# The tile of 32 overflow rows in a routed feed-forward: its row load, its place among the experts, and a down product in four column tiles

## The chip, the cores and the metric

The kernel runs on one core of one Trainium2 chip. The metric is the device time in microseconds of one execution of the whole program. Before the change three runs gave a median of 414.18 us (413.87 to 414.41).

## What is computed

A decoder layer on 8 sequences of 112 tokens with 256 channels: self attention, cross attention on 375 context tokens, and a feed-forward in which each token goes to one of 8 experts beside a shared part. Layer norms follow each sum. All is float32. Cut to the part at hand:

```python
logits = x_ @ router.T
idx = jnp.argmax(logits, axis=-1)
onehot = jax.nn.one_hot(idx, 8)
u = jnp.einsum('bc,ehc->ebh', x_, up)
g = jnp.einsum('bc,ehc->ebh', x_, gate)
ye = jnp.einsum('ebh,ech->ebc', jax.nn.silu(g) * u, down)
y = jnp.einsum('ebc,be->bc', ye, onehot)
ys = jax.nn.silu(x_ @ w_gate_s.T) * (x_ @ w_up_s.T) @ w_down_s.T
x = layernorm(x + y + ys)
```

Here x_ has 896 rows of 256, and the hidden size is 512.

## The kernel before

The two attentions take the first 318 us or so of the profiled execution and are not touched. Then comes the feed-forward, whose order is written out by hand in the table LAST: a string of short words, each of which is a function that issues a few instructions. Every engine runs its own instructions in that order, so the table is the order of each queue. The pool of each tile name has a fixed number of buffers, and a new tile waits until the oldest of its name is free.

**The experts.** The rows of x are scattered to a DRAM array xs_d in which each expert owns a stretch of 896 rows; xs_d is filled by indirect DMAs. Each expert's first 128 rows make a tile (tiles 0 to 7). Rows beyond 128 of one expert are few: with at most 32 of them, of one expert, they make tile 8, a `SmallTile` of 32 rows, whose expert (`whose_i`) and first row (`row_i`) VectorE works out (`beyond`, the word x). With more rows the program goes into a tail under a condition, which this input does not take.

Each tile has three pieces:

- `turn` (words A0 to A8, line 820): two PE transposes of its rows, and a copy by ScalarE.
- `gate_up` (B0 to B8): 16 matmuls for gate and up, then silu on ScalarE and a product on VectorE, which gives hT. For tile 8 (line 862) the rows are the stationary side, and the four quarters of the hidden size go to four column tiles of PE, at output partitions 0, 32, 64 and 96.
- `down` (C0 to C8): four matmuls that add up in PSUM, then VectorE adds x (line 850), and SP writes the rows to a DRAM array y_d (line 851). For tile 8 the hidden part is first turned by one transpose (line 876) and a ScalarE copy (hTs, line 878).

`down(t)` also calls `load_expert(t + 4)`: SP issues the three weight loads of the tile four places on (wg, wu, wd, lines 600 to 602, 512 KB each, four buffers each). For tile 8 SP first loads `whose_i` and `row_i` into registers (line 805), then issues the load of the 32 rows (line 894), then the weights of that expert. All these DMAs stand on SP's one queue, in order.

**After the experts.** i0 writes the place of every token to DRAM, and i1 reads it back in another layout (line 694). Y0 to Y6 gather y_d by these places with indirect DMAs on GpSimd (line 697); Y0 waits for all writes to y_d. g0 and g1 are silu and product of the shared part's two halves (lines 639 and 640), h3 is a last piece of it. D0 to D6 are the down products of the shared part, of 128 tokens each: four matmuls, the gathered rows added by VectorE (line 648), and the statistics of the norm. They take turns with two PSUM buffers. Z0 to Z6 apply the norm on ScalarE and write the result.

`ident` is a 128x128 unit matrix, made by GpSimd at the start.

Of the kernel before, what the change touches and what calls it, by code (L numbers as in the profile page):

```python
# [8 lines left out]
F32 = mybir.dt.float32  # L9
I32 = mybir.dt.int32  # L10
AF = mybir.ActivationFunctionType
ALU = mybir.AluOpType
AX = mybir.AxisListType

P = 128
# [29 lines left out]
LAST = """  # L45
S0 a2- E0 a1+ S1 T00+ T01- E1 b0- T02+ S2 F1 T10- W0 T12- E2 b1- U0+ T11+ S3 T20+ T21- a0- F2 E3
T22+ W1 V0 F3 T30- T32- F4 T31- U1- r V1 f1 R a3- f2 b2+ f3 f4 p h2 P b3- h1 L0 L1 g0 h0 A0 x A1 L2
B0 i0 B1 C0 A2 C1 A3 B2 A4 B3 C2 A5 B4 C3 C4 A6 B5 A7 B6 A8 C5 B7 C6 B8 C7 g1 i1 C8 Y0 h3 Y1 Y2 Y3
D0 Y4 Y5 D1 Y6 D2 Z0 D3 D4 Z1 D5 Z2 Z3 Z4 D6 Z5 Z6
"""  # L50


# [1 line left out]
def decoder_layer(  # L54
# [8 lines left out]
    nc = tc.nc  # L63
    B, S, D = x.shape
    NT = B * S
# [8 lines left out]
    E, _, H = upT.shape  # L74
    KH = H // P
# [6 lines left out]
    SMALL = 32  # L82

    const = ctx.enter_context(tc.tile_pool(name="const", bufs=1))
# [4 lines left out]
    V, A, G = nc.vector, nc.scalar, nc.gpsimd  # L89
# [4 lines left out]
    def t_tile():  # L94
        return ps_t.tile([P, 512], F32, tag="pt", name="pt")

    def m_tile():
        return ps_m.tile([P, 512], F32, tag="mm", name="mm")
# [25 lines left out]
    load = nc.sync.dma_start  # L124
# [53 lines left out]

    ident = const.tile([P, P], F32, name="ident")
    make_identity(nc, ident)  # L180
    mhalf = const.tile([P, 1], F32, name="mhalf")
    G.memset(mhalf, -0.5)

# [28 lines left out]
    xs_d = tc.dram_tile([E * NT, D], F32, name="xs_d")  # L212
    y_d = tc.dram_tile([E * NT, D], F32, name="y_d")
# [42 lines left out]
    def product(out_, pairs):  # L256
        for i, (lhsT, rhs) in enumerate(pairs):
            nc.tensor.matmul(out_, lhsT, rhs, start=(i == 0), stop=(i == len(pairs) - 1))  # L258
# [313 lines left out]
    for s in range(B):  # L572
        if s + 1 < B:
            load_context(s + 1)
        if s in (1, 2):
            load(
                out=(xs_d if s == 1 else y_d)[:, :].rearrange("(t p) d -> p t d", p=P),
                in_=fill_sb.unsqueeze(1).to_broadcast([P, E * NT // P, D]),
# [14 lines left out]
    fp = ctx.enter_context(tc.tile_pool(name="fp", bufs=2))  # L593
    wp = ctx.enter_context(tc.tile_pool(name="wp", bufs=4))

    def load_weights(u, g, d):
        wg = wp.tile([P, KD, H], F32, tag="wg", name="wg")
        wu = wp.tile([P, KD, H], F32, tag="wu", name="wu")
        wd = wp.tile([P, KH, D], F32, tag="wd", name="wd")
        load(out=wg, in_=g.rearrange("(k p) h -> p k h", p=P))  # L600
        load(out=wu, in_=u.rearrange("(k p) h -> p k h", p=P))
        load(out=wd, in_=d.rearrange("(k p) c -> p k c", p=P))
        return wu, wg, wd
# [38 lines left out]
    def last_sum(i):  # L642


        h, n = (raw["u"], i) if i < FT else (hS1, i - FT)
        ps = m_tile()
        product(ps[:, :D], [(h[:, hc, bass.ts(n, P)], swd[:, hc, :]) for hc in range(KH)])
        V.tensor_tensor(r[:, i, :], ps[:, :D], r[:, i, :], ALU.add)
        stats(mv[:, i, :], r[:, i, :])
        rstds[i] = rstd_of(mv[:, i, 1:2])  # L650

    def last_norm(i):
        shift = mv[:, i, 0:1]
        V.tensor_scalar(shift, shift, rstds[i], -1.0, ALU.mult, ALU.mult)
        A.activation(r[:, i, :], r[:, i, :], AF.Identity, bias=shift, scale=rstds[i])
        load(out=out[bass.ts(i, P), :], in_=r[:, i, :])

    raw_pieces = {}
# [3 lines left out]
    def small_tile(name, shape=None, dt=F32):  # L662
        return fc.tile(shape or [S, B], dt, name=name)
# [26 lines left out]
    def places_out():  # L690
        load(out=place_d[:, :].rearrange("(b s) o -> s (b o)", s=S), in_=place_i)

    def places_in():
        load(out=place_2, in_=place_d[:, :].rearrange("(i p) o -> p (i o)", p=P))

    def from_places(i):
        G.indirect_dma_start(
            out=r[:, i, :],
            out_offset=None,
            in_=y_d[:, :],  # L700
            in_offset=bass.IndirectOffsetOnAxis(ap=place_2[:, i : i + 1], axis=0),
            bounds_check=E * NT - 1,
            oob_is_err=False,
        )
# [50 lines left out]
    row_i = small_tile("row_i", [1, NOV], I32)  # L755
# [48 lines left out]
    def value(at, most):  # L804
        return nc.sync.value_load(at, min_val=0, max_val=most)
# [4 lines left out]
    class ExpertTile:  # L810
# [32 lines left out]
        def down(self):  # L843
            ps = m_tile()
            n = self.x.shape[0]
            product(
                ps[:n, :D], [(self.hT[:, hc, 0:n], self.w[2][:, hc, :]) for hc in range(KH)]
            )
            y = fp.tile([P, D], F32, tag="y", name="y", bufs=3)
            V.tensor_tensor(y[:n], ps[:n, :D], self.x, ALU.add)  # L850
            load(out=y_d[bass.ds(self.rows, n), :], in_=y[:n])

    class SmallTile(ExpertTile):
# [17 lines left out]
            V.tensor_tensor(h, ug[:, 0, 0:P], h, ALU.mult)  # L871
            self.h = h

        def down(self):
            pt = t_tile()
            nc.tensor.transpose(pt[:, 0:P], self.h, ident)
            self.hT = fp.tile([P, KH, SMALL], F32, tag="hTs", name="hTs", bufs=1)
            A.copy(self.hT.rearrange("p k n -> p (k n)"), pt[:, 0:P])
            super().down()

    tiles = [ExpertTile(t * NT, xs[:, t, :]) for t in range(E)]
    tiles.append(SmallTile(None, xs[0:SMALL, E, :]))
# [5 lines left out]
    def load_expert(t):  # L888
        if t < E:
            tiles[t].w = load_weights(upT[t], gateT[t], downT[t])  # L890
        else:
            e = value(whose_i[0:1, 0:1], E - 1)
            tiles[t].rows = value(row_i[0:1, 0:1], E * NT - P)
            load(out=tiles[t].x, in_=xs_d[bass.ds(tiles[t].rows, SMALL), :])
            tiles[t].w = load_weights(upT[e], gateT[e], downT[e])

    for t in range(4):
        tiles[t].w = weights.pop(t)

    def down(t):  # L900
        tiles[t].down()
        if t + 4 <= E:
            load_expert(t + 4)
# [7 lines left out]
    for t in range(E + 1):  # L911
        raw_pieces[f"A{t}"] = lambda on, t=t: tiles[t].turn()
        raw_pieces[f"B{t}"] = lambda on, t=t: tiles[t].gate_up()
        raw_pieces[f"C{t}"] = lambda on, t=t: down(t)
    raw_pieces["i0"] = lambda on: places_out()
    raw_pieces["i1"] = lambda on: places_in()
    for i in range(NTT):
        raw_pieces[f"Y{i}"] = lambda on, i=i: from_places(i)
        raw_pieces[f"D{i}"] = lambda on, i=i: last_sum(i)
        raw_pieces[f"Z{i}"] = lambda on, i=i: last_norm(i)  # L920
# [79 lines left out]
```

## Time and profile before

| what | value |
|---|---|
| median of three runs | 414.18 us (413.87 to 414.41) |
| the profiled execution | 414.01 us |
| its span in the trace | 412.2 us |
| granted TensorE clock, mean | 0.995 |
| busy: PE, VectorE, ScalarE, GpSimd | 398.8, 235.9, 194.0, 73.4 us |
| share of PE in the chain that ended last | 84% |
| tile 5's gate product starts / ends | 367.34 / about 369.13 us |
| last down product of the experts ends | 388.5 us |
| last instruction that is counted as busy starts | 406.18 us |

The times in the last three rows are from the start of the span. In the timeline a line gives the start in us, the length in us, the engine, the line of the code, the instruction, the tile that it writes and those it reads, shapes and the number of records; in brackets stands the time for which the engine was idle just before, and what released it. A float32 matmul leaves two records. PE is the matmuls and PEld the weight loads. An engine with a q behind its name is that engine's queue of DMA issues; the length is that of the issue, not of the transfer. The end of a transfer is given apart, as the time from issue to landing. The chain that ended last is followed back from the last instruction, at each step to what released it.

### The profile page before, as it was taken

What the parts mean: (1) busy time and instruction counts of PE and PEld (TensorE: products, weight loads), DVE (VectorE), ACT (ScalarE), POOL (GpSimd) and SP (SyncE); (2) the same over time, 40 slices, a digit from 0 to 9 for tenths busy, and PEclk for the clock granted to TensorE, in tenths of its full rate; (3) what the DMA queues carried; (4) which work ended last, traced back from release to release, by engine and by line L of the source; (5) the groups of instructions that cost most, each with busy time, mean ns of one, the idle gap of its engine ahead of it and who ended that gap; (6) DMA issues with size and microseconds to landing.
All of it is one profiled execution on the core that took longest, in us unless ns stands there. A gap on an engine that the chain in (4) does not pass through costs nothing.

```text
span 412.2 us, 8511 instructions
## 1 busy us (share of the span) xinstructions
PE 398.8 (97%) x3353; PEld 312.1 (76%) x3353; DVE 235.9 (57%) x665; ACT 194.0 (47%) x486; POOL 73.4 (18%) x109
## 2 busy tenths in 40 slices
PE   8999999999999999999999999999999999999991
PEld 8877768867886887688678867867857559998681
DVE  1164685588458666855784586489567533211362
ACT  1242475356636554654557286677468331201203
POOL 3030012113012200221030113104101440000082
PEclk9999999999999999999999999999999999999998
DMA  7990497199010001000000100000596132977133
GB/s 249 311 254 2 150 369 237 42 378 330 4 40 0 2 2 39 0 2 13 27 2 2 39 0 3 1 2 2 179 376 213 32 114 57 322 258 255 31 89 96
DMA packets 40382, 46.61 MB, mean 113 GB/s; under 512 B 4005, under 2 KB 33458, under 8 KB 40338
## 3 DMA queue, kind: packets, MB, share of 16 engines
q1 hardware_dynamic: 39074, 43.93, 33.2%
q0 software_dynamic: 720, 1.84, 1.5%
q8 instruction: 28, 0.46, 0.4%
q10 hardware_dynamic: 544, 0.26, 0.2%
q14 instruction: 16, 0.13, 0.1%
HBM read 28.42 MB, written 17.60 MB: 112 GB/s over the span
## 4 chain that ended last, share of the span: by engine, by line
PE 84%; DMA 6%; issue 3%; POOL 2%; SPq 1%; DVE 1%; ACT 1%; POOLq 0%; DVEq 0%
PE mm L258 47%; PE pt L495 10%; PE sc L447 7%; PE mm L506 4%; PE sc L258 4%; PE sc L346 4%; PE mm L382 3%; PE pt L375 3%; DMA xs<-xs_d 2%; POOL xs_d L675 1%; DMA wk<-in_w_qkv 1%; DMA wu<-in_upT 1%; PE pt L249 1%; DMA r<-y_d,place 1%; DMA xs_d<-xres,place_i 1%
## 5 line engine op out<-in xcount | busy, mean ns | idle before, releaser
L465 ACT ACTIVATE ex<-ex,nm 112x375 f32<-112x375 f32 x128 | 76.5, 599 | 48.8 <-DVE nm L461 48.0
L461 DVE CUSTOM_DVE_ANT_0 ex<-sc,cap 112x375 f32<-112x375 f32 x128 | 63.7, 543 | 10.1 <-PE sc L447 9.3
L495 PEld LDWEIGHTS pt<-ident,ex 112*125 112x125 f32 x384 | 50.8, 188 | 17.1 <-issue 9.2
L495 PE MATMUL pt<-ident,ex 112*125 112x112 f32 x384 | 55.4, 276 | 0.1
L254 ACT COPY exT<-pt 125x448 f32<-125x448 f32 x58 | 29.4, 526 | 26.1 <-PE pt L495 25.9
L368 POOL TENSOR_TENSOR pr<-pr,den 112x896 f32<-112x896 f32 x16 | 26.9, 1683 | 78.5 <-DVE den L367 41.8
L239 POOL TENSOR_TENSOR rs<-rs,mhalf 112x1 f32<-112x1 f32 (+1 forms) x23 | 12.7, 552 | 151.9 <-DVE rs L238 151.4
L258 PE MATMUL mm<-wv,xT_sb 128*112 128x512 f32 x64 | 31.1, 608 | 0.0
L447 PE MATMUL sc<-kc,qz 32*112 32x375 f32 x256 | 29.8, 519 | 0.1
L258 PE MATMUL mm<-wo,aoT 128*112 128x256 f32 x128 | 29.0, 380 | 0.0
L258 PE MATMUL mm<-xT_sb,wq 128*128 128x224 f32 x128 | 27.9, 363 | 0.0
L254 DVE COPY exT<-pt 125x448 f32<-125x448 f32 x38 | 23.6, 622 | 6.3 <-PE pt L495 5.8
L258 PE MATMUL mm<-xT_sb,wk 128*128 128x224 f32 x128 | 26.9, 354 | 0.3 <-DMA wk<-in_w_qkv 0.3
L258 PEld LDWEIGHTS mm<-xT_sb,wq 128*128 128x128 f32 x128 | 24.0, 195 | 3.3 <-issue 3.2
L258 PE MATMUL mm<-wxv,cT 128*125 128x256 f32 x96 | 25.6, 389 | 0.0
L258 PEld LDWEIGHTS mm<-wo,aoT 128*112 128x112 f32 x128 | 22.0, 177 | 4.5 <-DVE aoT L254 0.2
L258 PEld LDWEIGHTS mm<-xT_sb,wk 128*128 128x128 f32 x128 | 23.7, 190 | 2.0 <-PE mm L258 0.6
L465 ACT ACTIVATION_READ_ACCUMULATOR ex<-ex,nm 112x1 f32 x128 | 23.9, 187 | 0.0
L258 PE MATMUL mm<-cT,wxk 128*128 128x375 f32 x64 | 23.2, 486 | 0.0
L506 PE MATMUL mm<-exT,vc 125*32 125x112 f32 x768 | 21.7, 261 | 0.0
L254 DVE COPY prT<-pt 112x448 f32<-112x448 f32 x16 | 9.8, 620 | 20.7 <-PE pt L375 20.7
L355 DVE TENSOR_REDUCE mx<-sc 112x8 f32<-112x896 f32 x16 | 17.4, 1088 | 5.9 <-PE sc L346 5.4
(160 smaller groups left out, 645.0 us busy)
## 6 DMA issues: line engine op xcount, KB each, us to landing
xs_d<-fill_sb SPq DMA_DIRECT2D x1, 7168.0 KB, 24.0
y_d<-fill_sb SPq DMA_DIRECT2D x1, 7168.0 KB, 24.7
wg<-in_gateT SPq DMA_DIRECT2D x9, 512.0 KB, 6.4
wu<-in_upT SPq DMA_DIRECT2D x9, 512.0 KB, 7.3
wd<-in_downT SPq DMA_DIRECT2D x9, 512.0 KB, 8.8
cT<-in_ctxT SPq DMA_DIRECT2D x8, 375.0 KB, 3.3
wv<-in_w_qkv SPq DMA_DIRECT2D x2, 512.0 KB, 8.2
wo<-in_w_out SPq DMA_DIRECT2D x1, 1024.0 KB, 13.6
```

Source lines behind the costliest of these rows:

```text
L239: G.tensor_tensor(rs[:n], rs[:n], mhalf[:n], ALU.pow)
L254: (V.tensor_copy if on == "+" else A.copy)(dst, src)
L258: nc.tensor.matmul(out_, lhsT, rhs, start=(i == 0), stop=(i == len(pairs) - 1))
L346: nc.tensor.matmul(sc[:S, j, bass.ts(c, S)], qT[rows, 4 * g + c, self.tok], kT[rows, 4 * g + c, self.tok], start=True, stop=True,)
L355: V.tensor_reduce(self.mx, scv, AX.X, ALU.max)
L368: G.tensor_tensor(pr, pr, den.unsqueeze(3).to_broadcast([S, 2, 4, S]), ALU.mult)
L375: nc.tensor.transpose(pt[:S, bass.ts(c, S)], self.pr[g][:, j, c, :], ident[:S, :S])
L447: nc.tensor.matmul(sc[i // 2][:S, i % 2, :S2], self.qz[rows, par, c, :], kc[rows, c, :], start=True, stop=True,)
L461: V.tensor_tensor_reduce(ex[:, i, :], self.sc[g][i // 2][:S, i % 2, :S2], cap, -1.0, BIG, ALU.add, ALU.min, nm[:, i : i + 1],)
L465: A.activation(ex[:, i, :], ex[:, i, :], AF.Exp, bias=nm[:, i : i + 1], scale=-1.0, accum_out=den[:, i, g % 2 : g % 2 + 1],)
L495: nc.tensor.transpose(pt[:JT, bass.ts(i, S)], self.ex[g][:, i, bass.ts(t, JT)], ident[:S, :S])
L506: nc.tensor.matmul(av[32 * i : 32 * i + 32, 0:S], vcs[self.b % 2][:, t, 4 * c + i, bass.ds(32 * par, 32)], self.exT[2 * c + par][:, t, bas ...
```

## The change

Four things are changed, all of them on tile 8, and one word of the shared part moves with them.

1. The load of the 32 rows, with the register load of `row_i`, is a word of its own, L3, behind C0.
2. In the table, A8 goes ahead of B6 and B8 ahead of C6; the turn of the hidden part is a word of its own, y0, behind C6; g1 goes behind A8, and i1 ahead of C7.
3. The down product of tile 8 is the word y1, between B7 and C7. Its four matmuls no longer add up in one PSUM area of 32 rows: each goes to its own 32 output partitions. ScalarE copies the four parts to a tile of the name y.
4. C8 is one matmul that adds up the four parts, with a 0/1 matrix of 128x32 (`fourth`) which VectorE makes at the start by adding up four column blocks of `ident`. Its sum has x added and is written as before.

```diff
-B0 i0 B1 C0 A2 C1 A3 B2 A4 B3 C2 A5 B4 C3 C4 A6 B5 A7 B6 A8 C5 B7 C6 B8 C7 g1 i1 C8 Y0 h3 Y1 Y2 Y3
-D0 Y4 Y5 D1 Y6 D2 Z0 D3 D4 Z1 D5 Z2 Z3 Z4 D6 Z5 Z6
+B0 i0 B1 C0 L3 A2 C1 A3 B2 A4 B3 C2 A5 B4 C3 C4 A6 B5 A8 g1 B6 C5 A7 B8 C6 y0 B7 y1 i1 C7 C8 Y0 h3
+Y1 Y2 Y3 D0 Y4 Y5 D1 Y6 D2 Z0 D3 D4 Z1 D5 Z2 Z3 Z4 D6 Z5 Z6
...
+    fourth = const.tile([P, 32], F32, name="fourth")
+    V.tensor_reduce(fourth, ident.rearrange("p (c m) -> p m c", m=32), AX.X, ALU.add)
...
-        def down(self):
+        def turn_hidden(self):
             pt = t_tile()
             nc.tensor.transpose(pt[:, 0:P], self.h, ident)
             self.hT = fp.tile([P, KH, SMALL], F32, tag="hTs", name="hTs", bufs=1)
             A.copy(self.hT.rearrange("p k n -> p (k n)"), pt[:, 0:P])
-            super().down()
+
+        def down_parts(self):
+
+            ps = m_tile()
+            for hc in range(KH):
+                nc.tensor.matmul(
+                    ps[32 * hc : 32 * hc + 32, :D], self.hT[:, hc, :], self.w[2][:, hc, :],
+                    start=True, stop=True,
+                )
+            self.parts = fp.tile([P, D], F32, tag="y", name="yp", bufs=3)
+            A.copy(self.parts, ps[:, :D])
+
+        def down(self):
+            ps = m_tile()
+            nc.tensor.matmul(ps[:SMALL, :D], fourth, self.parts, start=True, stop=True)
+            y = fp.tile([P, D], F32, tag="y", name="y", bufs=3)
+            V.tensor_tensor(y[:SMALL], ps[:SMALL, :D], self.x, ALU.add)
+            load(out=y_d[bass.ds(self.rows, SMALL), :], in_=y[:SMALL])
...
             e = value(whose_i[0:1, 0:1], E - 1)
-            tiles[t].rows = value(row_i[0:1, 0:1], E * NT - P)
-            load(out=tiles[t].x, in_=xs_d[bass.ds(tiles[t].rows, SMALL), :])
             tiles[t].w = load_weights(upT[e], gateT[e], downT[e])
...
+    def load_beyond():
+        tiles[E].rows = value(row_i[0:1, 0:1], E * NT - P)
+        load(out=tiles[E].x, in_=xs_d[bass.ds(tiles[E].rows, SMALL), :])
+
+    raw_pieces["L3"] = lambda on: load_beyond()
...
+    raw_pieces["y0"] = lambda on: tiles[E].turn_hidden()
+    raw_pieces["y1"] = lambda on: tiles[E].down_parts()
```

## The prediction

> **What bounds the kernel now.** I read the page's busy shares first: PE is busy for 398.8 of 412.2 us. A busy share is a mean over stages, so I then read the chain that ended last, cut to the stage that the change touches (from 360 us), and last the timeline of that stage, first PE alone, then all engines.
>
> PE's timeline, whose columns are start, length, engine and line, instruction, and the idle time before it. "x16" counts records, two for each fp32 matmul:
>
> ```profile
> 375.82 0.28 PE L820 MATMUL pt<-ident,xs 32*128 32x32 f32 x2 [0.95 <-DMA xs<-xs_d]
> 376.03 1.99 PE L258 MATMUL mm<-wd,hT 128*128 128x256 f32 x8
> 377.86 1.95 PE L258 MATMUL sc<-xsT,wg 128*128 128x128 f32 x16
> ...
> 381.43 1.89 PE L258 MATMUL mm<-wd,hT 128*128 128x256 f32 x8
> 383.25 0.65 PE L862 MATMUL sc<-wg,xsT 128*32 128x128 f32 x16
> 383.71 0.62 PE L862 MATMUL sc<-wu,xsT 128*32 128x128 f32 x16
> 384.26 1.99 PE L258 MATMUL mm<-wd,hT 128*128 128x256 f32 x8
> 386.09 0.27 PE L876 MATMUL pt<-ident,h 128*128 128x128 f32 x1
> 386.72 1.91 PE L258 MATMUL mm<-wd,hTs 128*32 128x256 f32 x8 [0.35 <-ACT hTs L878]
> 388.56 1.56 PE L258 MATMUL sc<-x2T,swu 128*128 128x384 f32 x4
> ```
>
> The differences of the starts are what each piece costs PE: an expert's gate and up 3.57, its down product 1.73 to 1.83, a turn 0.21, the small tile's gate 0.46 and up 0.55, its down product 1.84. PE stands still for 0.95 (the 32 rows) and 0.35 us (the turned hidden rows). Both are taken away by the change.
>
> But PE is not what ends this stage. The chain, whose columns are start, length and what:
>
> ```profile
> 389.11 1.49 DMA y_d<-y
> ...
> 391.56 2.82 DMA r<-y_d,place
> ...
> 394.96 7.19 PE mm L258 x32
> ```
>
> After the last down product the chain leaves PE: VectorE adds x, the 32 rows are written (landed 390.60), GpSimd gathers, VectorE adds (to 394.92), and only then does PE get a PSUM buffer for the third sum (D2) (394.96). PE fills that time with h3, D0 and D1 and idles just 0.15 us. So an earlier PE is worth nothing unless the write of the small tile's rows **lands** earlier; I work out that landing.
>
> The links on both sides of it, from the timeline of all engines:
>
> ```profile
> 381.63 0.60 ACT L839 ACTIVATE sg<-sc 128x512 f32<-128x512 f32 x1 [5.23 <-PE sc L258]
> 382.26 0.69 DVE L841 TENSOR_TENSOR hT<-sc,sg 128x512 f32<-128x512 f32 x1 [3.77 <-ACT sg L839]
> ...
> 386.75 0.33 SPq L851 DMA_DIRECT2D y_d<-y  x1
> ...
> 388.67 0.41 DVE L850 TENSOR_TENSOR y<-mm,xs 32x256 f32<-32x256 f32 x1 [0.82 <-PE mm L258]
> ```
>
> An expert's hidden rows are ready 1.57 us after PE ends its up product (381.43 to 382.95, and 0.05 to start); before, C6 (1.82) covered this for B7.
>
> **The change, part by part.** PE's order after B5, which ends at 370.92, becomes A8, B6, C5, A7, B8, C6, y0, B7, y1, C7, C8.
>
> Removed: the 0.95 and the 0.35 us. The rows' load, with its register load, moves from SP's queue ahead of tile 8's weights to behind C0's. There SP is idle until C2's write at 360.53 apart from C1's write and tile 5's weights; these go 1.4 us later (the same items took SP from 369.86 to 371.28). Tile 5's last landings are 359.5 (up) and 360.9 (down); PE wants them from 367.34. Cost nothing; without that cover, 1.4. g1 moves ahead of B6: ScalarE 1.05 and VectorE 1.22 us between 371.9 and 374.2, where before both idle from 372.4 to 374.9; nothing, or up to 1 us on hT6, which C6 wants only after 377. The 0/1 matrix is one VectorE instruction near 1.5 us, of some 0.3 by the nearest small rows (h, 128x128: 0.29); VectorE then idles 6.57 us until 8.63: nothing. The place load goes ahead of C7's write; it took 2.4 us and has more time than before.
>
> The down product in four column tiles: 8 records of 256 columns. The nearest row is L862, where 16 records of 128 columns in four column tiles took 0.46 to 0.55: so about 0.5, and 1.84 if the tiles ran one after another. With the sum (one matmul, two records at 0.216: 0.43) 0.93 in place of 1.84. The Trainium skill (TensorEngine Tiling (Array Packing), Key Properties) speaks against it: a change of tiling mode drains the array. The row: around L862 weight loads idle 0.33 and 0.20. By the row and the rule alike y1 may be 0.5 longer, 1.0 in all, and it still ends inside the wait that follows, so the sum does not move.
>
> **New wait 1: tile 8's up weights.** B8 comes 6.6 us earlier (376.65 for 383.25), its weights hardly do:
>
> ```profile
> L601 SPq DMA_DIRECT2D wu<-in_upT x1: 378/378/378, 372.2 to 372.2; - x1
> ...
> DMA to landing us min/median/max: 6.8/6.8/6.8
> ```
>
> 372.17 + 6.8 = 378.97, and B8's up half wants them at 377.11. SP issues them 1.4 us sooner (the second register load and the rows' DMA are gone). If landing followed issue: 377.55. If it follows the backlog of the queue: 378.97 less 0.08 for the 32 KB: 378.9. The small transfers say backlog: the 128 KB y at 368.82 landed after 6.7 us and the 32 KB rows, at 370.73, after 4.95, against 1.5 to 1.8 elsewhere. In half-microsecond windows the DMA share was 0.54 to 0.62 from 369.5 to 371 and 0.53 at 373, so an earlier issue can fill a little. I take 378.5, near the backlog's end; PE starts 0.14 after a landing (375.68 to 375.82): a wait of 378.64 - 377.11 = 1.53, bounds 0 (the transfers run at the full rate seen later, 390 GB/s) and 1.93. Behind it on PE stand C6, y0, B7 and all the rest.
>
> **New wait 2: hT7.** Between B7 and C7 only y1 (0.5) is left to cover 1.57: 1.07 us idle.
>
> **New wait 3: the small tile's write behind C7's.** The rows' place is a register, so the write can overlap any other; the changed program makes SP wait for the landing of C7's write (its semaphore stands in the write's list of waits). It did so before too, but then C7's write at 386.75 had landed after 1.8, at 388.55, 0.5 us before the small y was ready at 389.08. Now C7 ends only 0.43 before the small product: the two landings follow one another. The skill (DMA: Bandwidth & Descriptors, Two DMAs through the same engine are not ordered) says that this wait cannot be dropped, and (Anatomy of one DMA, fitted on GpSimd's path) that each transfer has about 2.0 us fixed: by the rule the second landing costs 2.08, by the row 1.49. I use the row; the rule would add 0.6.
>
> **Sum.** A8 371.13, B6 374.71, C5 376.44, A7 376.65, B8's gate 377.11, wait to 378.64, up 379.19, C6 381.02, y0 381.23, B7 384.80, hT7 at 386.37, C7 388.17, small sum 388.60 (before: 388.56). The 2.2 us taken off PE are given back as waits. Then y7: 388.17 + 0.2 + 0.42 + 0.04 = 388.83 issued, + 1.8 = 390.63 landed; small write + 0.2 (SP's moves) = 390.83, + 1.49 = 392.32 landed, against 390.60. **+1.7 us.** The gather and all after it follow unchanged: third sum (D2) at 396.7. The profiled execution took 414.01 us (span 412.2 and 1.8 around it): 415.7. The median of the runs, 414.18, becomes 415.9.
>
> **The rivals.** (a) The weights come in time (full DMA rate). Then C7 ends at 386.64, the small write lands at 390.8: +0.2, 414.4. For it: 390 GB/s at 376 to 378. Against it: 133 to 250 GB/s at 370.5 to 373.5.
> (b) Faster: the small write is not held back by C7's (it lands before, or the wait is not on it) and weights come in time. Then 387.07 + 0.18 + 0.42 + 0.04 + 1.49 = 389.2: -1.4, 412.8. It decides once the two writes overlap in full and the wait for weights is under 0.6. Against it: the semaphore in the list.
> (c) Slower still: full backlog (+0.4), and the second write takes 1.8 like its neighbours (+0.3): 416.6.
> (d) The column tiles do not run side by side: y1 1.84 ends 0.3 after hT7: 416.2, inside the forecast.
>
> **Chances.** Measurement tells about 0.2% (0.83 us) from no change. Forecast with (d) 0.58, of which nearly all is slower; (a) 0.25, same; (b) 0.05, faster; (c) 0.12, slower. So slower 0.68, same 0.28, faster 0.04. The range runs from (a) less 0.3 of scatter (runs before span 0.54 us) to just above (c).
>
> **What would show it.** The 0.95 and 0.35 idle times gone; PE idle ahead of L865's second half, put to DMA wu; about 1.1 us ahead of C7 on hT; the small y_d write starting some 2 us after C7's, not after its own y; about 1.8 us of PE idle ahead of the third sum (D2). Wrong would be: no wait for wu8 (then 414.4), or a small write issued beside C7's.

## The result, and the profile after

The change makes the kernel slower, by about a quarter of a per cent. Nine runs of the changed kernel gave a median of 415.31 us (414.89 to 415.94), and nine of the kernel before, on the same chip, 414.18 us: a ratio of 1.0027 with a 95% interval of 1.0015 to 1.0038, so +1.1 us (0.6 to 1.6). The profiled execution took 415.78 us with a span of 414.0, which is +1.77 on the profiled execution of before. The forecast was +1.7, inside the range; why the profiled pair shows nearly all of it and the medians only two thirds is the main thing that the experiments had to settle.

PE's timeline of the changed kernel, in the stage that the change touches (columns as before; L865 is tile 8's gate and up, L879 the turn of its hidden rows, L887 the down product in four column tiles, L896 the sum of the parts):

```profile
371.08 0.31 PE L823 MATMUL pt<-ident,xs 32*128 32x32 f32 x2
...
376.72 0.38 PE L823 MATMUL pt<-ident,xs 128*128 128x128 f32 x2
377.57 0.64 PE L865 MATMUL sc<-wg,xsT 128*32 128x128 f32 x16 [0.47 <-ACT xsT L827]
378.85 0.64 PE L865 MATMUL sc<-wu,xsT 128*32 128x128 f32 x16 [0.63 <-DMA wu<-in_upT]
379.43 1.99 PE L261 MATMUL mm<-wd,hT 128*128 128x256 f32 x8
...
385.03 0.64 PE L887 MATMUL mm<-wd,hTs 128*32 128x256 f32 x8
386.51 1.99 PE L261 MATMUL mm<-wd,hT 128*128 128x256 f32 x8 [0.84 <-DVE hT L844]
388.44 0.62 PE L896 MATMUL mm<-yp,fourth 128*32 128x256 f32 x2
388.99 1.56 PE L261 MATMUL sc<-x2T,swu 128*128 128x384 f32 x4
...
396.68 3.50 PE L261 MATMUL mm<-swd,raw_u 128*128 128x256 f32 x15 [1.39 <-DVE r L651]
```

The waits for the rows (0.95) and for the turned hidden rows (0.35) are gone, and three others are there: at B8 for weights, 0.84 ahead of C7, and 1.39 ahead of the third sum (D2), where PE stood still for 0.09 before (from 394.87 to 394.96; the prediction's 0.15 is a little large). h3 starts at 388.99; it started at 388.56 before. So what PE was relieved of has been given back by the time it reaches h3. How long the wait at B8 is can't be read from its brackets alone. From the turn at 376.72 to C6 at 379.43 it is 2.71 us, and 1.32 in executions without any wait there (shown below): 1.39 us.

The chain that ended last, of the same execution:

```profile
370.54 8.27 DMA wu<-in_upT
...
386.51 2.01 PE mm L261 x8
388.52 0.02 issue
388.55 0.43 DVE y L853
388.98 0.02 issue
389.00 1.70 DMA y_d<-y
...
390.91 1.50 DMA y_d<-y
...
393.28 2.82 DMA r<-y_d,place
...
396.68 7.19 PE mm L261 x32
```

Here is the loss. Two landings stand one behind the other: C7's 128 rows (389.00 to 390.70), then the 32 rows, issued only at 390.91, although VectorE had them ready (the add of line 898 started at 389.10 and took 0.41). They land at 392.41; before they landed at 390.60. Gather, add and D2 follow.

### The profile page after: what moved, and what is told of

Read it like the earlier page. It is cut to its first block, busy times and chain, and to the rows that moved or that the text cites. A ratio compares the mean times of both kernels' runs of the same rounds, so it can differ in the third digit from the quotient of the medians.

```text
span 414.0 us, 8520 instructions
## 1 busy us (share of the span) xinstructions
PE 398.9 (96%) x3355; PEld 312.2 (75%) x3355; DVE 236.3 (57%) x666; ACT 194.5 (47%) x487; POOL 73.4 (18%) x109
## 3 DMA queue, kind: packets, MB, share of 16 engines
q0 software_dynamic: 720, 1.84, 1.5%
## 4 chain that ended last, share of the span: by engine, by line
PE 85%; DMA 5%; issue 3%; POOL 2%; DVE 1%; SPq 1%; ACT 1%; POOLq 0%; DVEq 0%
PE mm L261 47%; PE pt L498 10%; PE sc L450 7%; PE sc L261 5%; PE mm L509 4%; PE sc L349 4%; PE mm L385 3%; PE pt L378 3%; DMA wu<-in_upT 2%; POOL xs_d L678 1%; PE mm L136 1%; DMA y_d<-y 1%; PE pt L252 1%; DMA r<-y_d,place 1%; DMA xs_d<-xres,place_i 1%
```

## The experiments

The theory: the loss is made by the wait for hT7 and the two landings in sequence, and what PE saves lies behind the gather and is worth nothing. The first rival: the late weights of tile 8 make it. The second: the down product in parts and its sum make it.

For each trace I use one length, **the stage**: from the start of tile 5's gate product to the start of D2. It is 396.68 - 367.41 = 29.27 us in the changed kernel and 394.96 - 367.34 = 27.62 before. What follows it, from D2 to the start of the last counted instruction, takes 11.21 or 11.22 us in every trace of this document, so nothing of the change is lost or won there.

**Tile 8's weights ahead of tile 7's.** SP issues the two sets of weight loads in the other order, so that tile 8's come sooner and tile 7's later:

```diff
-            load_expert(t + 4)
+            load_expert({3: 8, 4: 7}.get(t, t + 4))
```

> The changed kernel, but tile 8's weights are asked for after C3 and tile 7's after C4, the other way round. Theory of three waits: the 0.47 and 0.63 us for which PE idles ahead of the two halves of B8 are waits for tile 8's weights; they go, the small write lands 1.1 us earlier (about 391.3 in place of 392.4), time 415.3 - 1.1 = 414.2. Tile 7's up weights then land at about 378.8, ahead of B7 at 380.2. Rival (the weights cost nothing that ends later; the time is lost in the early load or in the column tiles): 415.3. Rival (the 0.47 ahead of the gate half is for the copy of A7, not for weights): only 0.6 comes back, 414.7.

Measured: 415.01 us, 1.0023 (1.0013 to 1.0033) against before. From PE's timeline of this kernel:

```profile
376.74 0.38 PE L823 MATMUL pt<-ident,xs 128*128 128x128 f32 x2
377.05 0.64 PE L865 MATMUL sc<-wg,xsT 128*32 128x128 f32 x16
377.51 0.62 PE L865 MATMUL sc<-wu,xsT 128*32 128x128 f32 x16
378.06 1.99 PE L261 MATMUL mm<-wd,hT 128*128 128x256 f32 x8
...
385.15 1.99 PE L261 MATMUL mm<-wd,hT 128*128 128x256 f32 x8 [0.84 <-DVE hT L844]
```

B8 does not wait (378.06 - 376.74 = 1.32), nor does B7 for tile 7's weights, yet the time stayed about where it was: 0.2 us less than the changed kernel by the two ratios, with some 0.6 either way. The expectation missed. The first rival can't be the main cause: with no wait for weights at all the kernel is still 0.95 us slower than before.

**The small rows written to a fixed place.** The address is then no register, and SP does not have to wait for C7's write. The last 32 rows of y_d, which C7's write does not touch, take the rows, so this kernel leaves tile 8 out of the result.

```diff
-            load(out=y_d[bass.ds(self.rows, SMALL), :], in_=y[:SMALL])
+            load(out=y_d[E * NT - SMALL : E * NT, :], in_=y[:SMALL])
```

> The changed kernel, but the small tile's 32 rows go to a fixed place, the last 32 rows of y_d, so that its write need not wait for C7's; the rows of tile 8 are left out of the result. Theory of three waits: the small write is issued at about 389.55 in place of 390.91 and lands by 391.1 to 391.3 in place of 392.4; time 415.3 - 1.2 = 414.1. Rival (the two writes lie beside each other anyway, or the gather waits for something else): 415.3.

Measured: 414.21 us, 1.0008 (1.0000 to 1.0016), some 0.8 us less than the changed kernel. The chain of this kernel:

```profile
388.33 0.56 PE mm L896 x2
388.89 0.02 issue
388.91 0.42 DVE y L898
389.33 0.02 issue
389.35 1.48 DMA y_d<-y
```

The write goes out as soon as its own add is done, 0.53 us behind C7's (388.82), and one landing of 1.48 is left in the chain. PE does not idle ahead of D2. The wait that the prediction named is real: the edit takes it away, with SP's register moves for the address (0.2 us), and touches nothing else. The wait of 0.84 for hT7 is still there. The run also refutes the prediction's rival (b): that the write isn't held back.

**The sum and its write ahead of C7.** The same remedy with the whole result kept; one word moves in the table:

```diff
-... C6 y0 B7 y1 i1 C7 C8 Y0 h3
+... C6 y0 B7 y1 i1 C8 C7 Y0 h3
```

> The changed kernel, but the small sum and its write (C8) stand ahead of C7 in the table; the column tiles stay. Theory of three waits: the sum lies in the 0.84 us for which PE waits for hT7, the small write lands at about 388.8, and C7's, which now comes last, at about 390.9 in place of 392.4: 1.5 us less than the changed kernel of the same call. Rival (the order of the two writes does not matter, only how much stands behind C7): about the same as the changed kernel, or 0.4 less for the sum that is hidden.

Measured: 413.88 us, 0.9994 (0.9983 to 1.0005), beside 1.0028 for the changed kernel, run again (below): -1.4 us, close to the 1.5 expected. PE's timeline:

```profile
383.49 0.64 PE L887 MATMUL mm<-wd,hTs 128*32 128x256 f32 x8
384.62 0.62 PE L896 MATMUL mm<-yp,fourth 128*32 128x256 f32 x2 [0.49 <-ACT yp L892]
385.17 1.99 PE L261 MATMUL mm<-wd,hT 128*128 128x256 f32 x8
```

SP's two writes, from the timeline of all engines (L899 the 32 rows, L854 C7's):

```profile
385.71 0.34 SPq L899 DMA_DIRECT2D y_d<-y  x1
...
387.65 0.34 SPq L854 DMA_DIRECT2D y_d<-y  x1
```

The sum (0.55) stands where PE waited for hT7, so that wait is gone, and the small write has landed long before C7's is issued. One landing is left, C7's. The edit undoes waits 2 and 3 together.

**Only the early rows.** The kernel before, with the rows' load as a word behind C0 and nothing else:

```diff
-B0 i0 B1 C0 A2 C1 ...
+B0 i0 B1 C0 L3 A2 C1 ...
```

> The kernel before, with one part of the change alone: the 32 rows and their register load behind C0. Theory of three waits: the 0.95 us of PE idle at A8 goes and nothing new comes, since B8 stays late (about 382.3, its weights there by 379), C8 keeps its place, and C7's write has landed before the small y is ready: 414.2 - 0.95 = 413.2. Rival (the early load costs SP's queue or the transfers what it brings): 414.2.

Measured: 413.27 us, 0.9990 (0.9982 to 0.9998): -0.41 us, less than half of the 0.95 of the profiled execution. In the trace the rows are waited for no more and nothing else is late. So the 0.95 is not what an execution pays on average.

**Both kernels again.** 

> The changed kernel once more, as the measure for the others of this call. Expected 1.0027 of before as in its first runs. If it comes out nearer 1.0038, the upper end of that interval, the swap of the weights and the other single edits had gained more than their medians seemed to say.

> The kernel before once more, for a trace of the same call. The time from the last counted instruction to the end of the span was 6.0 us in its first trace and 6.3 to 6.8 in those of the single edits. If it is 6.3 to 6.8 here, that is a difference of chips or of executions, not of the edits; if it is 6.0 again, an earlier end is partly given back by the last stores.

Measured: 415.24 us (1.0028, 1.0018 to 1.0037) and 413.84 us (0.9994, 0.9980 to 1.0008). A second trace of the same programs answers what the early rows left open. From PE's timeline, first the kernel before:

```profile
373.39 1.95 PE L258 MATMUL sc<-xsT,wu 128*128 128x128 f32 x16
375.34 0.28 PE L820 MATMUL pt<-ident,xs 32*128 32x32 f32 x2
```

and the changed one:

```profile
377.06 0.38 PE L823 MATMUL pt<-ident,xs 128*128 128x128 f32 x2
377.37 0.64 PE L865 MATMUL sc<-wg,xsT 128*32 128x128 f32 x16
378.01 0.64 PE L865 MATMUL sc<-wu,xsT 128*32 128x128 f32 x16
378.59 1.99 PE L261 MATMUL mm<-wd,hT 128*128 128x256 f32 x8
...
385.68 1.99 PE L261 MATMUL mm<-wd,hT 128*128 128x256 f32 x8 [0.84 <-DVE hT L844]
...
395.85 1.35 PE L261 MATMUL mm<-swd,raw_u 128*128 128x256 f32 x5 [1.39 <-DVE r L651]
```

The 0.95 is gone: the rows landed 3.8 us after their issue, not 5.0. The wait at B8 has shrunk from 1.39 to 1.53 - 1.32 = 0.21: the up weights landed after 7.2 us, not 8.3. The 0.84 and the 1.39, on the other hand, are the same to 0.01 us. **Two kinds of wait have been mixed**: those for transfers at 370 to 379 us, which come and go from execution to execution, and those that the order makes, which stand in each. What the second trace of before was meant to tell came out too: from the start of the last counted instruction to the end of the span it was 6.0 us in the first trace and is 6.6 here, in the range of the single edits (6.3 to 6.8), so it differs between two executions of one program as much as between edits.

**Only the order.** The changed kernel's order up to B7, without parts: tile 8's down product adds up in PSUM as before, and C8 is ahead of C7.

```diff
-... C6 y0 B7 y1 i1 C7 C8 Y0 h3
+... C6 y0 B7 i1 C8 C7 Y0 h3
...
-            nc.tensor.matmul(ps[:SMALL, :D], fourth, self.parts, start=True, stop=True)
+            product(
+                ps[:SMALL, :D], [(self.hT[:, hc, :], self.w[2][:, hc, :]) for hc in range(KH)]
+            )
```

> The changed kernel's order with the down product of before: in place of y1 stands the small tile's whole down product (four matmuls that add up, no parts, no 0/1 sum), so its write goes ahead of C7's. Theory of three waits: 1.84 us of PE work covers the wait for hT7 in full, C7 ends at about 388.6 as now, but the small write lands at about 389 and C7's, behind it, at 390.95 in place of 392.4: 415.3 - 1.45 = 413.9, so the column tiles and their sum at the end are a loss. Rival (the column tiles save PE time that counts): more PE work, 415.3 + 0.9 = 416.2.

Measured: 413.96 us, 1.0007 (0.9998 to 1.0015). It is 0.9 us faster than the changed kernel, less than the 1.45 expected. PE's timeline:

```profile
383.95 1.91 PE L261 MATMUL mm<-wd,hTs 128*32 128x256 f32 x8
385.80 1.99 PE L261 MATMUL mm<-wd,hT 128*128 128x256 f32 x8
```

C7 does not wait; tile 8's product of 1.85 us covers hT7 by itself. B8 waited 0.77 us for weights in this trace.

**Only the parts.** The order before, with y0, y1 and the sum one behind the other after C7:

```diff
-... C0 L3 A2 ... A6 B5 A8 g1 B6 C5 A7 B8 C6 y0 B7 y1 i1 C7 C8 Y0 h3
+... C0 A2 ... A6 B5 A7 B6 A8 C5 B7 C6 B8 C7 g1 i1 y0 y1 C8 Y0 h3
...
             e = value(whose_i[0:1, 0:1], E - 1)
+            load_beyond()
```

> The kernel before in its own order, with one part of the change alone: the small tile's down product on four column tiles, the parts copied by ScalarE and added up by the 0/1 matrix, all behind C7. Theory: 0.64 for the parts, 0.49 of PE idle for the copy (as in front of the sum in the kernel with the sum first) and 0.55 for the sum stand in place of 1.84, so the small write lands 0.1 to 0.2 us earlier: the same as before within 0.2. Rival (the column tiles give their full saving, 1.84 - 0.93): 0.9 less than before. Rival (the copy on the path costs more than is saved): 0.4 more.

Measured: 414.07 us, 1.0002 (0.9989 to 1.0014), no difference. PE's timeline:

```profile
387.17 0.64 PE L887 MATMUL mm<-wd,hTs 128*32 128x256 f32 x8 [0.35 <-ACT hTs L881]
388.30 0.62 PE L896 MATMUL mm<-yp,fourth 128*32 128x256 f32 x2 [0.49 <-ACT yp L892]
388.85 1.56 PE L261 MATMUL sc<-x2T,swu 128*128 128x384 f32 x4
```

From 387.17 to 388.85 it is 1.68 us, beside 1.84 for the product that adds up. The four column tiles run side by side (0.64 in all), but the copy of the parts (0.49) and the sum (0.55) eat nearly all of it. The prediction's rival (d) falls. So does the second rival, in the changed order too: sum first (parts) and order only (no parts) both have the write of the 32 rows ahead of C7's, and the stage, without the wait at B8, is 26.42 us with parts and 26.59 without.

**Swap and sum first together.** The two edits of the first and third experiment in one kernel, run twice:

> As the kernel with the sum first, and tile 8's weights asked for ahead of tile 7's. If the waits for weights count in full, 1.1 to 1.4 us less than the kernel with the sum first. If, as the swap alone suggested by its median, they do not, the same as that one within 0.3.

> The kernel with the swap of weights and the sum first once more, beside the last one on the same chip. Its first ratio was 0.9975 [0.9963, 0.9988], that of the covered kernel 0.9985 [0.9976, 0.9994]; their traces put the third sum of the shared part within 0.15 us of each other. Expected between the two, 0.998.

Measured: 413.30 us, 0.9975 (0.9963 to 0.9988), and 413.18 us, 0.9978 (0.9969 to 0.9987). This is the version that beats both: about 1.0 us less than before, about 2 less than the changed kernel. On the kernel with the sum first it gains 0.7 to 0.8, between the two forecasts (1.1 to 1.4, or nothing beyond 0.3). Of PE's waits only the one ahead of D2 (0.48) and that for the parts (0.49) are left.

**hT7 covered by work.** The swap, tile 8's product without parts, and B7 ahead of C6, so that two down products stand between B7 and C7:

```diff
-... A8 g1 B6 C5 A7 B8 C6 y0 B7 y1 i1 C7 C8 Y0 h3
+... A8 g1 B6 C5 A7 B8 B7 y0 C6 i1 C8 C7 Y0 h3
```

> All three waits taken away: rows early, tile 8's weights ahead of tile 7's, B7 right behind B8, then C6 (it covers hT7), the small tile's down product in one piece (no column tiles), and C7 and its write last. Theory of three waits: no idle on PE to the end of C7 at about 386.9, its write lands at 389.2 against 390.6 before, third sum of the shared part 1.4 earlier against a before with the 0.95 wait for the rows, 0.5 to 1.0 earlier against one without: 1.0 to 1.4 less than before, and less than the kernel with the swap and the sum first by 0.2 or so. Rival (the end is set by the transfers of the last stores, which grow as the rest ends earlier): no more than 0.5 less than before.

Measured: 413.34 us, 0.9985 (0.9976 to 0.9994). PE does not idle until D2. Faster than before by 0.6, which is less than expected and near the rival's 0.5, and not to be told from the kernel above by its interval.

**The same with the weights in their usual order,** and B8 late enough for them; hT has three buffers for it, and sg gives one up (two), since with three of each the pool `wp` would want 48 KB per partition where 46.03 are left:

```diff
-... A8 g1 B6 C5 A7 B8 C6 y0 B7 y1 i1 C7 C8 Y0 h3
+... A8 g1 B6 A7 B7 B8 C5 y0 C6 i1 C8 C7 Y0 h3
```

> As the covered kernel, but with the weights asked for in their usual order and B8 put behind B7 (C5 and C6 behind both), so that tile 8's weights have until about 378.5 to land; hT has three buffers and sg two. Theory of three waits: PE has the same work as the covered kernel and idles 0.3 us at most ahead of B8: within 0.3 of 0.9985 of before. If B8 waits there, up to 0.5 more.

Measured: 414.20 us, 1.0007 (0.9997 to 1.0017), a miss. PE's timeline:

```profile
374.76 0.38 PE L823 MATMUL pt<-ident,xs 128*128 128x128 f32 x2
375.88 2.05 PE L261 MATMUL sc<-xsT,wg 128*128 128x128 f32 x16 [0.73 <-ACT xsT L827]
```

B8 waits for no weights, but tile 7's turn now stands right ahead of its own gate product: ScalarE's copy of the turned rows, which other pieces used to cover, is exposed, and it starts only at 375.46, since ScalarE takes tile 6's silu first (from 374.96). From turn to gate it is 1.12 us instead of the 0.31 of a turn.

## Why the prediction came out as it did

All traces in one table. "Transfer wait" is the time at A8 for the rows, or at B8 for the weights (A7's start to C6's start, less 1.32); the fourth column is the stage without it. The time against before is worked out from the ratio. Where D2's first record follows D1's without a gap, its start is taken from the chain.

| kernel | stage, us | transfer wait | stage less wait | time against before, us |
|---|---|---|---|---|
| before, two traces | 27.62, 26.67 | 0.95, 0 | 26.67, 26.67 | |
| changed, two traces | 29.27, 28.10 | 1.39, 0.21 | 27.88, 27.89 | +1.1, +1.2 |
| weights swapped | 27.87 | 0 | 27.87 | +0.95 |
| fixed place | 27.84 | 1.29 | 26.55 | +0.3 |
| sum first | 26.61 | 0.19 | 26.42 | -0.25 |
| rows early | 26.55 | 0 | 26.55 | -0.4 |
| order only | 27.36 | 0.77 | 26.59 | +0.3 |
| parts only | 27.81 | 1.23 | 26.58 | +0.1 |
| swap and sum first, two traces | 26.44, 26.42 | 0, 0 | 26.44, 26.42 | -1.0, -0.9 |
| hT7 covered | 26.63 | 0 | 26.63 | -0.6 |
| hT7 covered, weights in order | 27.53 | 0 | 27.53 | +0.3 |

The fourth column repeats to 0.02 us in the three programs that were traced twice: what the order makes is the same in both. By it the change costs 27.88 - 26.67 = 1.21 us. To that comes the mean of one transfer wait less that of the other.

Point by point:

- **Direction and mechanism: right.** The prediction said that PE's saving is given back as waits, and that the small write lands later because the two landings follow one another. Two edits that undo this, each in its own way, shorten the stage less wait by 1.33 (fixed place) and 1.46 us (sum first). The first leaves the wait for hT7 in and still comes below before (26.55 and 26.67), so the loss goes with the second landing alone. What the wait for hT7 costs while two landings follow is not shown: no run takes it away alone.
- **New wait 3: right in size.** The first landing took 1.70 (taken: 1.8), the second 1.50 (1.49). The Trainium skill's fixed cost of about 2.0 us for each transfer (DMA: Bandwidth & Descriptors, Anatomy of one DMA) would, as an estimate, have made the second 2.08; the row was the better guide.
- **New wait 2: right, a little large.** 0.84 in place of 1.07, in all four traces with this order. hT7 came when the sum had it, 5.14 us after B7's start, but y1 began 0.09 later behind B7 (3.66 us for 3.57) and took 0.64 and not 0.5. For the drain at a change of tiling mode, which the skill names without a price (TensorEngine Tiling (Array Packing), Key Properties), the prediction allowed y1 up to 1.0; nothing of that size is seen, the 0.09 and the 0.14 together being 0.23.
- **New wait 1 and the 0.95 removed: the step that failed.** In the execution that was profiled the working holds: 1.39 us at B8 (predicted 1.53, all of it ahead of the up half; 0.54 of it stood ahead of the gate half), the small rows landed at 392.41 (392.32), D2 at 396.68 (396.7), the execution at 415.78 (415.7). But the sum then added the +1.7 of one execution to the median of all. It took the rows' 0.95 out of before and put 1.53 for the weights in, a net of +0.58, as if both were constants. Second traces show 0 and 0.21, and that the first pair of executions came within 0.1 us of the forecast is in part luck: the second pair ran 414.07 and 415.25, which is +1.18.

  All traces together give a fairer mean. Five have the changed order and the usual order of loads as far as B8 (both of the changed kernel, fixed place, sum first, order only): their wait for the weights is 0.77 in the mean. Three have the rows' load in its old place (both of before, parts only): 0.73. As an estimate from these eight, the two waits nearly cancel, and the change comes to 1.21 + 0.04 = 1.25 us; measured are +1.1 (0.6 to 1.6). The run times are less sharp. By them the rows are worth some 0.3 us (rows early: -0.41, of which 0.12 is in the stage less wait), and the weights 0.2 (swap against the changed kernel) to 0.8 (swap and sum first against sum first), each with 0.3 to 0.7 either way.
- **Rival (a), weights in time, +0.2:** wrong in its number for the same reason. From the start of the stage, the small rows land after 23.61 us with swapped weights. Against the first trace of before, with its 0.95, that is 0.35 later (23.26), near what (a) gave; against the second, without it, 1.30 later (22.31). The kernel with weights in time measured +0.95.
- **Early load and g1: right.** SP's queue has tile 5's weights later and PE does not wait for them, and neither hT6 nor the rows are waited for.

What stays open: ahead of the stage and behind the last counted instruction executions differ as well. The stage starts between 366.95 and 367.81, and from the start of that instruction to the end of the run it is 7.83 to 8.54 us. In the two traces of before this hides the 0.95: the second began the stage 0.47 later and took 0.55 more at the end (8.38 for 7.83), and the two ran 414.01 and 414.07. No run here takes either apart. Whether the end grows when the rest is done sooner is not shown: the two traces of swap and sum first, with stages alike to 0.02, have 8.40 and 8.04.

Some edits also gained less than the stage says. With the mean waits above, weights swapped, fixed place, rows early and order only fall 0.3 to 0.5 us short, all others 0.2 or less. These four were timed beside one set of runs of before, with a median of 413.74 where the other sets have 413.96 to 414.25. That before waited less for its rows in that set would explain it, but it was not traced there.

## What to carry to other kernels

Ask when the last write lands, not when its engine ends: a write to an address from a register waits here for the write to the same array issued ahead of it (issued at 390.91, behind a landing at 390.70; at 389.35 with a fixed address), so it belongs well ahead of the last one, or it costs a whole landing. When a piece is moved, ask for both sides what it covered (C6 covered hT7; B8 and C6 covered A7's copy) and whether its loads come as much earlier as it does. A wait for a transfer in one profiled execution is a sample, not a constant: take a second trace before it goes into a sum, and take it out of the comparison if it comes and goes.

## What was not expected of the hardware

The same 512 KB load, at the same place of the same program, landed after 8.3 us in one execution and 7.2 in another, and its issue kept SP's queue for 1.41 and 0.53 us. The 32 rows took 5.0 and 3.8 us in the kernel before, while 32 KB writes with little else under way took 1.48 to 1.50 in seven traces.

A releaser can be misnamed. In the first trace of the changed kernel the 0.47 us ahead of B8's gate product is put down to ScalarE's copy of the turned rows. In the trace with the fixed place, 0.37 us at the same point is put down to the gate weights, and in the second trace of the changed kernel and with swapped weights the gate product followed the turn without any wait. The copy was the same in all of them, 0.47 us behind the turn's start and 0.37 long, and it is that of tile 7's rows, which this product does not read. The gate weights, issued at 369.97, landed after 7.5 us, at about 377.5, and the product began at 377.57: the 0.47 is a wait for the weights.
